# A four-layer graph network on one core: tiles finished in fours, column sums on ScalarE, and shifted transposes around the last layer

## The chip, the cores and the metric

The kernel runs on 1 core of a Trainium2 chip. The metric is the device time of one execution, in microseconds (us). Three runs of the kernel before gave 3246.93, 3250.04 and 3250.78 us: the median is 3250.04. Lower is better.

The engines are called by the names of the profile: PE (TensorE, matmul; PEld is its weight load), DVE (VectorE), ACT (ScalarE), POOL (GpSimd) and SP (SyncE, which here only issues DMAs). Each engine works off its own queue in order.

## The reference

An input x of 3327 rows by 512 columns and a 3327 x 3327 adjacency matrix pass through four layers. Each layer adds its result to its input and normalises every row:

```python
x = _layernorm(x + _L0_gnn_ref(x, adj, W, a))   # attention, 8 heads of 64
x = _layernorm(x + _L1_gnn_ref(x, adj, ..., 64)) # mean over the first 64 neighbours, two linear maps
x = _layernorm(x + _L2_gnn_ref(x, adj, W, a))   # attention, 8 heads of 64, then elu
x = _layernorm(x + _L3_gnn_ref(x, adj, W, a))   # attention, 4 heads of 128, then elu
```

An attention layer projects x to Wh, takes for each head e[i, j] = leaky_relu(f1[i] + f2[j]) where adj[i, j] > 0, a softmax over j, and sums Wh[j] with these weights.

## The kernel before, in words

The 3327 rows are 26 tiles of 128 (NT = 26, the last one short by one row), in two halves of 13 tiles (HALF). The program is one stream of stages:

- the first projection (x times W of layer 0), during which most of the adjacency matrix is loaded as int32 and turned into a one-byte mask. The mask is made in pieces of 128 rows by 832 columns: `mask_load` (L885) issues the load from SP, `mask_set` (L894) makes the mask on DVE, or for some later ones on ACT. The pieces of the first half of the columns, and those of the second half for the first EARLY row tiles, belong to this stage (L1415, L1416); the others are made one by one during the first unit of the layer 0 attention, 4/3 of a step per row tile (`some`, L1494);
- the layer 0 attention (`attention8`), layer 1 (`sage`), the layer 2 attention (`attention8`);
- `third` (L1205): the layer 2 rows are finished and projected to layer 3, then the layer 3 attention (`attention`, `unit`) runs, with the finishing of the output as side jobs.

An attention unit loops over the 26 row tiles j: DVE makes t (L430 or L709), ACT makes y from it (L435 or L710), PE multiplies t with the values into `po` and y and the mask into `pd` (denominators). After the loop `po` is moved out to `ob`, and work on it is put in a list of jobs, of which the next unit takes one per row tile. At the end of three of layer 3's eight units (the fourth of the first half, the second and third of the second half) the denominators leave `pd` by four DVE block transposes (L529, L531), two DVE reduces (L535) and one store `dd` from SP; `place` (L540) loads them back in another layout by 16 small DMAs, and `finish_sums` (L555) makes the reciprocals `rec`.

Finishing rows (`finish_steps`, L167) works on a group of n tiles: a load of the attention's sums h and of the layer's input xr; for each tile a `divide` (h times `rec` on DVE, L183, and for an elu layer e = exp(h) on ACT, L190) and an `add` (two DVE instructions, L198 and L199); then `norm_rows` (L148) for the group: for each tile bn_stats and bn_aggr on DVE (L154, L155), one square root for the group on ACT (L156), one reciprocal and one product on DVE (L157, L160), and for each tile the scaling on ACT (L163). Each list of steps is called in the loop of `third`.

In that loop (L1236) the finished tile y is stored to x3 from SP, `project1` (L260) transposes it on PE into `pt`, ACT copies it to xT (L269), DVE sums the columns into xsum (L270, for the mean row used by the attention); `project2` (L273) of the tile before runs 16 matmuls into `pw`, and ACT and DVE take the result apart (rc, qc, dc, vt). Groups are of two tiles, loaded three groups ahead (`load_group`, L1226), with 10 buffers for h and 6 for xr. At tile 14 `prepare` (L306) and `cut` of the first half of layer 3 are put in. The layer 2 denominators come in by `L2.late`: `place` at tile 4, `finish_sums` at tile 8.

The order of PE's instructions is that of the program (L64). The order of the other engines' instructions is chosen when the program is built, by a planner with its own estimate of durations and landings: an instruction may be queued ahead of earlier written ones. `tc.keep_in_program_order(ins)` holds one instruction behind the one written just before it on the same engine. Pools with `bufs=k` rotate k buffers of one name; a tile waits until the one that had its buffer is no longer used.

Of the kernel before, what the change touches and what calls it, by code (L numbers as in the profile page):

```python
# [18 lines left out]
P = 128  # L19
# [13 lines left out]
def kernel(  # L33
# [23 lines left out]
    CUTS = ((0, WA // 2), (WA // 2, WA), (WA, WA + WB // 2), (WA + WB // 2, IW))  # L57
    assert WA // 2 <= 512
    PIECES = (0, 48, 72, 32)
    EARLY = 10  # L60
    QUADS = [(s, min(4, HALF - s)) for s in range(0, HALF, 4)]


# [81 lines left out]
            eng.dma_start(out=t[:, :, e, :FW], in_=src[:, e * FW:(e + 1) * FW].rearrange("(c p) m -> p c m", p=P))  # L145


    def norm_rows(pool, ys, t0):  # L148
        n = len(ys)
        st = pool.tile([P, 4, 6], F32, name="st")  # L150
        mv = pool.tile([P, 4, 2], F32, name="mv")
        rs = pool.tile([P, 4, 2], F32, name="rs")
        for s, y in enumerate(ys):
            nc.vector.bn_stats(out=st[:, s, :], in_=y)  # L154
            nc.vector.bn_aggr(out=mv[:, s, :], in_=st[:, s, :])  # L155
        nc.scalar.activation(rs[:, :n, 0], mv[:, :n, 1], AF.Sqrt, bias=eps)  # L156
        nc.vector.reciprocal(rs[:, :n, 0], rs[:, :n, 0])  # L157
        if t0 + n == NT:
            nc.vector.tensor_tensor(rs[:, n - 1, 0:1], rs[:, n - 1, 0:1], valid, op=ALU.mult)
        nc.vector.scalar_tensor_tensor(rs[:, :n, 1], mv[:, :n, 0], -1.0, rs[:, :n, 0],  # L160
                                       op0=ALU.mult, op1=ALU.mult)
        for s, y in enumerate(ys):
            nc.scalar.activation(y, y, AF.Identity, bias=rs[:, s, 1:2], scale=rs[:, s, 0:1])  # L163

    def finish_steps(pool, xin, layer, t0, n, hbufs=6, eng=nc.sync, xbufs=None, xpool=None, ebufs=None, pinned=False):  # L167
        H, D = layer.H, layer.D
        ys, xs, steps = [], [], []

        def load():
            for t in range(t0, t0 + n):
                xr = xpool.tile([P, F], F32, name="xr", tag="hb") if xpool else \
                    pool.tile([P, F], F32, name="xr", bufs=xbufs)
                h = pool.tile([P, F], F32, name="h", bufs=hbufs)
                load_tile(h, hd, t, eng)
                ys.append(h)
                load_tile(xr, xin, t, nc.gpsimd)
                xs.append(xr)

        def divide(s):
            h = ys[s]
            ins = nc.vector.tensor_tensor(h.rearrange("p (h d) -> p h d", h=H), h.rearrange("p (h d) -> p h d", h=H),  # L183
                                          rec[:, t0 + s, :H].rearrange("p (h e) -> p h e", e=1).to_broadcast([P, H, D]),
                                          op=ALU.mult)
            if pinned and t0 > 2:
                tc.keep_in_program_order(ins)
            if layer.elu:
                e = pool.tile([P, F], F32, name="e", bufs=ebufs)
                ins = nc.scalar.activation(e, h, AF.Exp)  # L190
                if pinned and layer.li == 2 and (t0, s) == (2, 0):
                    tc.keep_in_program_order(ins)
                xs.append(e)

        def add(s):
            h, xr = ys[s], xs[s]
            if layer.elu:
                nc.vector.scalar_tensor_tensor(xr, xs[n + s], 1.0, xr, op0=ALU.min, op1=ALU.add)  # L198
                nc.vector.scalar_tensor_tensor(h, h, 0.0, xr, op0=ALU.max, op1=ALU.add)  # L199
            else:  # L200
                nc.vector.tensor_tensor(h, h, xr, op=ALU.add)

        steps.append(load)
        if pinned:
            steps += [lambda s=s: divide(s) for s in range(n)] + [lambda s=s: add(s) for s in range(n)]
        else:
            for s in range(n):
                steps += [lambda s=s: divide(s), lambda s=s: add(s)]
        steps.append(lambda: norm_rows(pool, ys, t0))
        return ys, steps  # L210

    def finish(*a):
# [20 lines left out]
    class Layer:  # L233
# [25 lines left out]

        def project1(self, pool, ps, xt, t, blocks=False):  # L260
            xT = pool.tile([P, FC, P], F32, name="xT")
            if blocks:

                tc.keep_in_program_order(nc.vector.transpose(xT, xt))
            else:
                pt = ps.tile([P, FC, P], F32, name="pt")
                for c in range(FC):
                    nc.tensor.transpose(pt[:, c, :], xt[:, c * P:(c + 1) * P], ident)
                nc.scalar.copy(xT, pt)  # L269
            nc.vector.tensor_reduce(xsum[:, :, t], xT, AX.X, ALU.add)  # L270
            return xT
# [116 lines left out]
        def unit(self, pools, half, s, background, aside, final=None, ending=None, following=None):  # L388
# [135 lines left out]
            if not by_pe:  # L524


                end = half == 1 and s == NS - 1
                for c in range(2):
                    ins = nc.vector.transpose(db[:64, c * (WA // 2):(c + 1) * (WA // 2)], pd[c][:64, :WA // 2])  # L529
                    tc.keep_in_program_order(ins)  # L530
                    nc.vector.transpose(db[64:, c * (WB // 2):(c + 1) * (WB // 2)], pd[c][64:, :WB // 2])  # L531
                red = yp.tile([P, WA // 32, 2, NS], F32, name="red", tag="y")
                dv = db.rearrange("p (b s x) -> p b s x", s=NS, x=8)
                for o in range(2):
                    nc.vector.tensor_reduce(red[:, :, o, :], dv[:, :, :, 3 * o:3 * o + 3], AX.X, ALU.add)  # L535
                dd = dram.tile([P, WA // 32, 2 * NS], F32, name=f"dd{self.li}{half}{s}")
                nc.sync.dma_start(out=dd, in_=red.rearrange("p b o s -> p b (o s)"))
                held = []
# [12 lines left out]


                nc.vector.tensor_copy(rec[:, t0:t0 + HALF, hs], self.rc[:, t0:t0 + HALF, hs])

                def finish_sums():  # L555
                    pes = held[0]
# [15 lines left out]
                    return jobs  # L572
                if final and s > 1:

                    return [nothing, nothing, place, nothing, nothing, nothing, finish_sums] + jobs[2:]
# [629 lines left out]
    def third(first):  # L1205
        with tc.tile_pool(name="col3", bufs=1) as cp:
# [5 lines left out]
            with tc.tile_pool(name="p_w", bufs=1, reuse_waits="tile") as wp, \  # L1212
# [12 lines left out]

                def load_group(t0):  # L1226
                    if t0 < NT:
                        groups.append(finish_steps(fp, x2, L2, t0, 2, 10, nc.gpsimd if t0 < 4 else nc.sync, 6,
                                                    pinned=t0 == 2))
                        groups[-1][1].pop(0)()  # L1230

                load_group(2)
                load_wide(wsb, w3, nc.gpsimd)
                nc.vector.tensor_copy(wsb[:, :, :, FW:], wa[3].rearrange("p c (e h) -> p c e h", e=2))
                load_group(4)
                for t0 in range(0, NT, 2):  # L1236
                    ys = ahead
                    if t0 in (4, 8):
                        L2.late.pop(0)(fp)
                    load_group(t0 + 6)  # L1240
                    for s, y in enumerate(ys):
                        t = t0 + s
                        store_tile(x3, y, t, nc.sync)
                        xT = L3.project1(pp, ps, y, t)
                        if s == 0 and groups:
                            ahead, steps = groups.pop(0)
                            for f in steps:
                                f()
# [16 lines left out]
            with tc.tile_pool(name="f3", bufs=2) as fp, tc.tile_pool(name="f4", bufs=1) as gp:  # L1265
# [10 lines left out]
                def later(s):  # L1276
                    jobs = []
                    if s == 0:
                        jobs += [none] * 12
                        for t0 in range(0, HALF, 2):  # L1280
                            ys, steps = finish_steps(fp, x3, L3, t0, min(2, HALF - t0), 2)

                            def stores(ys=ys, t0=t0):
                                for q, y in enumerate(ys):
                                    store_tile(out, y, t0 + q, nc.sync)

                            jobs += steps + [stores]
# [111 lines left out]
    with tc.tile_pool(name="mask0", bufs=1, reuse_waits="tile") as mp0, \  # L1399
# [8 lines left out]
        with tc.tile_pool(name="p_w", bufs=1, reuse_waits="tile") as wp, \  # L1408
# [42 lines left out]
            for t in range(1, NT):  # L1451
                xT = L0.project1(pp, ps, load(t), t)
                L0.project2(pp, bank, wsb, *pend)
                pend = (xT, t)
                for _ in range(2 + (t % 3 == 1) if t < NT - 4 else 7):
                    if msteps:
                        msteps.pop(0)()
                if t == HALF + 1:
                    L0.prepare(pp, 0)
                    L0.cut(pp, 0)  # L1460
                if t == NT - 6:
                    L0.first_rows = L0.wide_rows(ring, UNITS[0])
# [115 lines left out]
```

## Time and profile before

| what | us |
|---|---|
| median of the runs (lowest, highest) | 3250.04 (3246.93, 3250.78) |
| the profiled execution, its own time | 3250.52 |
| its span, from the first instruction to the last | 3248.8 |
| PE busy in the span | 3139.2 (97%) |
| DVE busy | 2627.8 (81%) |
| ACT busy | 2286.6 (70%) |
| POOL busy | 233.5 (7%) |

The span by stages, with the busy time of the engines in each (from the windows of the trace):

| stage | from, to | length | PE | DVE | ACT |
|---|---|---|---|---|---|
| first projection | 0, 142 | 142 | 123.9 | 88.1 | 29.3 |
| layer 0 attention | 142, 945 | 803 | 795.3 | 780.1 | 714.1 |
| layer 1, projection of layer 2 | 945, 1613 | 668 | 654.9 | 369.5 | 257.4 |
| layer 2 attention | 1613, 2411 | 798 | 783.4 | 771.4 | 705.6 |
| last projection | 2411, 2551 | 140 | 117.5 | 113.0 | 102.9 |
| layer 3 attention | 2551, 3220 | 669 | 659.1 | 488.0 | 466.8 |
| last rows | 3220, 3249 | 29 | 5.2 | 17.8 | 10.5 |

How to read the profile: a page shows one execution; its busy times come from the hardware's record of each instruction. The slices cut the span in 40 parts of 81 us, each digit the busy share of an engine in tenths. A row of a timeline has the start, the length, the engine, the line, the operation, the operands, how many were merged, and in brackets how long the engine stood idle before it and which instruction ended that. A row of waits has who waited for whom, the sum in us, how often, and the longest. A row of windows has the stretch, its length and the busy time of each engine in it. A row of groups has line, engine, operation, operands, count, then busy us and mean ns, then idle time before. Matmuls are pipelined and their ends modelled, so a busy PE is not a PE at its best.

### The profile page before, as it was taken

What the parts mean: (1) busy time and instruction counts of PE and PEld (TensorE: products, weight loads), DVE (VectorE), ACT (ScalarE), POOL (GpSimd) and SP (SyncE); (2) the same over time, 40 slices, a digit from 0 to 9 for tenths busy, and PEclk for the clock granted to TensorE, in tenths of its full rate; (3) what the DMA queues carried; (4) which work ended last, traced back from release to release, by engine and by line L of the source; (5) the groups of instructions that cost most, each with busy time, mean ns of one, the idle gap of its engine ahead of it and who ended that gap; (6) DMA issues with size and microseconds to landing.
All of it is one profiled execution on the core that took longest, in us unless ns stands there. A gap on an engine that the chain in (4) does not pass through costs nothing.

```text
span 3248.8 us, 44852 instructions
## 1 busy us (share of the span) xinstructions
PE 3139.2 (97%) x17910; PEld 1601.2 (49%) x17910; DVE 2627.8 (81%) x2329; ACT 2286.6 (70%) x1817; POOL 233.5 (7%) x378
## 2 busy tenths in 40 slices
PE   8899999999999999999999999999988999999997
PEld 7644343333334467777633333333337655555453
DVE  5799999999977645555589999999989666677886
ACT  2398888899972334444488988899888655568886
POOL 3100000000010011111100000000011000010110
PEclk9999999999999999999999999999999999999998
DMA  9751114111134355555341111011137211122211
GB/s 365 263 175 52 43 53 154 40 42 41 33 110 125 96 136 133 141 132 153 93 134 45 42 35 38 20 42 41 32 107 244 80 43 43 44 57 89 85 42 52
DMA packets 354575, 300.07 MB, mean 92 GB/s; under 512 B 232420, under 2 KB 288174, under 8 KB 352831
## 3 DMA queue, kind: packets, MB, share of 16 engines
q1 hardware_dynamic: 322175, 185.92, 19.7%
q0 software_dynamic: 26672, 103.60, 10.1%
q10 hardware_dynamic: 5520, 7.69, 0.8%
q8 instruction: 141, 2.31, 0.3%
q14 instruction: 67, 0.55, 0.1%
HBM read 220.27 MB, written 76.84 MB: 91 GB/s over the span
## 4 chain that ended last, share of the span: by engine, by line
PE 81%; DVE 6%; issue 4%; DMA 4%; ACT 3%; POOL 0%; SPq 0%; POOLq 0%; DVEq 0%; ACTq 0%
PE po L731 35%; PE po L452 13%; PE acc L1171 9%; PE pd L687 7%; PE pw L278 6%; DVE t L709 3%; PE pz L1069 3%; PE pi L1072 3%; DMA raw<-in_adjT_dram 2%; PE pd L405 1%; PE pk L1040 1%; ACT y L435 1%; PE pt L751 1%; DVE t L430 1%; PE pe L793 1%
## 5 line engine op out<-in xcount | busy, mean ns | idle before, releaser
L710 ACT ACTIVATE y<-t,bi,sc 128x3328 fp8e4<-128x3328 f32 (+1 forms) x520 | 1337.4, 2603 | 105.0 <-PE pd L687 48.2
L731 PE MATMUL po<-t,vj 128*64 128x448 f32 (+1 forms) x6656 | 1276.2, 524 | 13.0 <-DVE t L709 12.0
L731 PEld LDWEIGHTS po<-t,vj 128*64 128x64 f32 x6656 | 457.7, 138 | 694.4 <-issue 631.0
L452 PE MATMUL po<-t,vj 128*128 128x448 f32 (+1 forms) x1664 | 601.8, 518 | 7.3 <-DVE ob L481 3.6
L430 DVE SCALAR_TENSOR_TENSOR t<-rba,qc,mk 128x1664 f32<-128x1664 f32 x208 | 403.4, 1946 | 131.0 <-PE po L452 97.6
L435 ACT ACTIVATE y<-t,bi,sc 128x1664 fp8e4<-128x1664 f32 x208 | 365.8, 1772 | 188.0 <-DVE t L430 174.2
L452 PEld LDWEIGHTS po<-t,vj 128*128 128x128 f32 x1664 | 312.0, 191 | 277.9 <-issue 172.8
L709 DVE SCALAR_TENSOR_TENSOR t<-rba,qc,mk 128x3328 f32<-128x3328 f32 (+1 forms) x130 | 379.6, 2987 | 12.8 <-DMA mk<-md 8.4
L709 DVE SCALAR_TENSOR_TENSOR t<-rbb,qc,mask 128x3328 f32<-128x3328 f32 (+1 forms) x130 | 380.0, 2984 | 10.2 <-PE po L731 7.2
L709 DVE SCALAR_TENSOR_TENSOR t<-rbb,qc,mk 128x3328 f32<-128x3328 f32 (+1 forms) x130 | 379.3, 2984 | 10.3 <-PE po L731 8.9
L709 DVE SCALAR_TENSOR_TENSOR t<-rba,qc,mask 128x3328 f32<-128x3328 f32 (+1 forms) x130 | 380.7, 2985 | 6.9 <-PE po L731 6.1
L1171 PE MATMUL acc<-zs,kt 128*128 128x512 f32 x1352 | 360.2, 420 | 0.0
L278 PE MATMUL pw<-wsb,xT 128*128 128x264 f32 (+1 forms) x1248 | 299.3, 395 | 10.3 <-DVE vt L284 8.2
L1171 PEld LDWEIGHTS acc<-zs,kt 128*128 128x128 f32 x1352 | 255.6, 189 | 52.2 <-PE pk L1022 0.8
L687 PE MATMUL pd<-y,sden 128*32 128x384 fp8e4 (+1 forms) x3328 | 271.6, 344 | 0.0
L278 PEld LDWEIGHTS pw<-wsb,xT 128*128 128x128 f32 x1248 | 239.9, 196 | 53.2 <-ACT xT L269 6.2
L1029 ACT CAST pk<-cy 128x512 f32<-128x512 bf16 x169 | 99.1, 587 | 221.4 <-DVE kt L1043 214.8
L1043 DVE SCALAR_TENSOR_TENSOR kt<-pk,mb 128x512 fp32r<-128x512 f32 x169 | 115.5, 684 | 116.7 <-PE pk L1040 115.5
L687 PEld LDWEIGHTS <-sden 128*32 128x32 bf16 x3328 | 89.7, 95 | 165.7 <-issue 150.1
L284 DVE TENSOR_TENSOR vt<-pw,dc 128x256 f32<-128x256 f32 x156 | 59.0, 417 | 71.1 <-ACT dc L279 66.0
L1069 PE MATMUL pz<-wn,xT 128*128 128x512 f32 x208 | 96.3, 607 | 5.7 <-DMA wn<-in_wnT_dram 5.4
L999 POOL DMA_DIRECT2D cy<-ctd x91 | 67.9, 746 | 368.1 <-ACT pk L1029 300.8
(221 smaller groups left out, 2080.1 us busy)
## 6 DMA issues: line engine op xcount, KB each, us to landing
raw<-in_adjT_dram SPq DMA_DIRECT2D x67, 416.0 KB
vj<-v SPq DMA_DIRECT2D x156, 128.0 KB
cy<-ctd POOLq DMA_DIRECT2D x78, 256.0 KB, 4.2
h<-hd SPq DMA_DIRECT2D x61, 256.0 KB
v<-vt SPq DMA_DIRECT2D x50, 256.0 KB
xr<-x POOLq DMA_DIRECT2D x45, 256.0 KB, 3.3
md<-mask SPq DMA_DIRECT2D x26, 416.0 KB
mb<-md SPq DMA_DIRECT2D x169, 64.0 KB
```

The costliest lines, as they stand in the source:

```text
L278: nc.tensor.matmul(pw[e][:, :FW + H], xT[:, c, :], wsb[:, c, e, :], start=c == 0, stop=c == FC - 1)
L430: ins = nc.vector.scalar_tensor_tensor(t, rb[k], self.qc[:, j, h:h + 1], mask_at[0](j, i0, IW), op0=ALU.max, op1=ALU.mult)
L435: nc.scalar.activation(y, t, AF.Sigmoid, bias=self.bi[:, j, h:h + 1], scale=self.sc[:, j, h:h + 1], saturate=False)
L452: nc.tensor.matmul(po[c][k * D:(k + 1) * D, :z - a_], vj[:, j % 2, k * D:(k + 1) * D], ts[k][:, a_:z], start=j == 0, stop=j == NT - 1)
L687: nc.tensor.matmul(pd[c][32 * kk:32 * kk + 32, :w_], lhsT, rhs, start=(kk, c) not in seen, stop=last and j == NT - 1)
L709: nc.vector.scalar_tensor_tensor(to, ro, self.qc[:, j, h:h + 1], m, op0=ALU.max, op1=ALU.mult)
L710: nc.scalar.activation(yo, to, AF.Sigmoid, bias=self.bi[:, j, h:h + 1], scale=self.sc[:, j, h:h + 1], saturate=False)
L731: nc.tensor.matmul(po[c][k * D:(k + 1) * D, :z - a_], vj[:, j % 2, x_:x_ + D], t[:, k, a_:z], start=j == 0, stop=j == NT - 1)
L1029: nc.scalar.copy(pks[k % 2], carry[b, t // 4 * 4][:, t % 4:t % 4 + 2, :])
L1043: nc.vector.scalar_tensor_tensor(kt, pk, NEIGHBOURS, mb[:, t:t + 2, :], op0=ALU.is_le, op1=ALU.mult)
L1069: nc.tensor.matmul(pz, xT[:, c, :], wn[:, c, :], start=c == 0, stop=c == FC - 1)
L1171: nc.tensor.matmul(acc, kts[b, t][:, s * P:(s + 1) * P], zs(t, c), start=t == 0 and c == 0, stop=t == NT - 1 and c == 1)
```

## The change

- `EARLY` goes from 10 to 8, so four mask pieces leave the first projection for the layer 0 attention; in the last four tiles of that stage the number of mask steps per tile goes from 7 to 4, 7, 4, 7.
- `norm_rows` can pin its reciprocal, and does so for tile 0 of layer 2. `divide` of layer 2 is pinned in every group called with `pinned`, which are now the groups at tiles 2 and 4 (before: an exp of the group at tile 2 alone).
- In `third` the tiles from 6 on are finished in groups of four, with all divides of a group written ahead of its adds (`together`), h in 14 buffers and xr in 12. A group's steps are spread over the first three tiles of the group before it. `place` and `finish_sums` of layer 2 are called at tiles 2 and 6.
- `project1` of layer 3 copies xT by four ACT instructions of 128 columns each, whose accumulator output is the column sum; the DVE reduce for xsum is gone there.
- In `unit` the block transposes of `pd`, the reduces and the store `dd` become the first two jobs of the next unit, without the pin, in place of two empty jobs.
- In the side jobs of the layer 3 attention the divides of a pair are written ahead of its adds.

The diff, cut to its core:

```diff
-    EARLY = 10
+    EARLY = 8
...
-    def norm_rows(pool, ys, t0):
+    def norm_rows(pool, ys, t0, pinned=False):
...
-        nc.vector.reciprocal(rs[:, :n, 0], rs[:, :n, 0])
+        ins = nc.vector.reciprocal(rs[:, :n, 0], rs[:, :n, 0])
+        if pinned:
+            tc.keep_in_program_order(ins)
...
-            if pinned and t0 > 2:
+            if pinned and (t0 > 2 or layer.li == 2):
                 tc.keep_in_program_order(ins)
...
-        if pinned:
+        if pinned or together:
             steps += [lambda s=s: divide(s) for s in range(n)] + [lambda s=s: add(s) for s in range(n)]
...
-        steps.append(lambda: norm_rows(pool, ys, t0))
+        steps.append(lambda: norm_rows(pool, ys, t0, t0 == 0 and layer.li == 2))
...
             xT = pool.tile([P, FC, P], F32, name="xT")
+            if self.li == 3:
+                pt = ps.tile([P, FC, P], F32, name="pt")
+                for c in range(FC):
+                    nc.tensor.transpose(pt[:, c, :], xt[:, c * P:(c + 1) * P], ident)
+                for c in range(FC):
+                    nc.scalar.activation(xT[:, c, :], pt[:, c, :], AF.Copy, accum_out=xsum[:, c, t:t + 1])
+                return xT
...
-                for c in range(2):
-                    ins = nc.vector.transpose(db[:64, c * (WA // 2):(c + 1) * (WA // 2)], pd[c][:64, :WA // 2])
-                    tc.keep_in_program_order(ins)
+                def blocks(c):
+                    nc.vector.transpose(db[:64, c * (WA // 2):(c + 1) * (WA // 2)], pd[c][:64, :WA // 2])
                     nc.vector.transpose(db[64:, c * (WB // 2):(c + 1) * (WB // 2)], pd[c][64:, :WB // 2])
...
+                jobs[:2] = [lambda: blocks(0), lambda: blocks(1)]
...
-                        groups.append(finish_steps(fp, x2, L2, t0, 2, 10, nc.gpsimd if t0 < 4 else nc.sync, 6,
-                                                    pinned=t0 == 2))
+                        groups.append(finish_steps(fp, x2, L2, t0, 2 if t0 < 6 else 4, 14, nc.gpsimd if t0 < 4 else nc.sync,
+                                                   12, pinned=t0 < 6, together=True))
...
                 load_group(4)
-                for t0 in range(0, NT, 2):
+                load_group(6)
+                t = -1
+                for t0 in (0, 2, 4, *range(6, NT, 4)):
                     ys = ahead
-                    if t0 in (4, 8):
+                    if t0 in (2, 6):
                         L2.late.pop(0)(fp)
-                    load_group(t0 + 6)
+                    load_group({2: 10, 4: 14}.get(t0, t0 + 12 if t0 >= 6 else NT))
+                    steps = []
+                    if groups:
+                        ahead, steps = groups.pop(0)
+                    per = -(-len(steps) // max(1, len(ys) - 1)) if len(ys) > 2 else len(steps)
                     for s, y in enumerate(ys):
                         t = t0 + s
                         store_tile(x3, y, t, nc.sync)
                         xT = L3.project1(pp, ps, y, t)
-                        if s == 0 and groups:
-                            ahead, steps = groups.pop(0)
-                            for f in steps:
-                                f()
+                        for f in steps[per * s:per * (s + 1)]:
+                            f()
...
-                            ys, steps = finish_steps(fp, x3, L3, t0, min(2, HALF - t0), 2)
+                            ys, steps = finish_steps(fp, x3, L3, t0, min(2, HALF - t0), 2, together=True)
...
-                for _ in range(2 + (t % 3 == 1) if t < NT - 4 else 7):
+                for _ in range(2 + (t % 3 == 1) if t < NT - 4 else 4 + t % 2 * 3):
```

More of the change, by code (lines that the diff above doesn't have):

```diff
@@ L163, in norm_rows, with finish_steps @@
             nc.scalar.activation(y, y, AF.Identity, bias=rs[:, s, 1:2], scale=rs[:, s, 0:1])
-    def finish_steps(pool, xin, layer, t0, n, hbufs=6, eng=nc.sync, xbufs=None, xpool=None, ebufs=None, pinned=False):
+    def finish_steps(pool, xin, layer, t0, n, hbufs=6, eng=nc.sync, xbufs=None, xpool=None, ebufs=None, pinned=False,
+                     together=False):
         H, D = layer.H, layer.D
@@ L527, in unit @@
                 end = half == 1 and s == NS - 1
-                for c in range(2):
-                    ins = nc.vector.transpose(db[:64, c * (WA // 2):(c + 1) * (WA // 2)], pd[c][:64, :WA // 2])
-                    tc.keep_in_program_order(ins)
+                dd = dram.tile([P, WA // 32, 2 * NS], F32, name=f"dd{self.li}{half}{s}")
+                held = []
+                def blocks(c):
+                    nc.vector.transpose(db[:64, c * (WA // 2):(c + 1) * (WA // 2)], pd[c][:64, :WA // 2])
                     nc.vector.transpose(db[64:, c * (WB // 2):(c + 1) * (WB // 2)], pd[c][64:, :WB // 2])
[L532 to L538, printed above, removed]
+                    if c == 0:
+                        return
+                    red = yp.tile([P, WA // 32, 2, NS], F32, name="red", tag="y")
+                    dv = db.rearrange("p (b s x) -> p b s x", s=NS, x=8)
+                    for o in range(2):
+                        nc.vector.tensor_reduce(red[:, :, o, :], dv[:, :, :, 3 * o:3 * o + 3], AX.X, ALU.add)
+                    nc.sync.dma_start(out=dd, in_=red.rearrange("p b o s -> p b (o s)"))
+                    nc.vector.tensor_copy(rec[:, t0:t0 + HALF, hs], self.rc[:, t0:t0 + HALF, hs])
+                jobs[:2] = [lambda: blocks(0), lambda: blocks(1)]
                 def place(eng=nc.gpsimd):
@@ L550, in place @@
                                 tc.keep_in_program_order(ins)
-                nc.vector.tensor_copy(rec[:, t0:t0 + HALF, hs], self.rc[:, t0:t0 + HALF, hs])
                 def finish_sums():
@@ L573, in unit @@
                 if final and s > 1:
-                    return [nothing, nothing, place, nothing, nothing, nothing, finish_sums] + jobs[2:]
+                    return jobs[:2] + [place, nothing, nothing, nothing, finish_sums] + jobs[2:]
                 jobs += [nothing] * max(0, 7 - len(jobs))
```

## The prediction

> **What bounds the kernel now.** I read the slices first, then a table of windows by stage, then TensorE's waits, then the timelines where it waits. From the page:
>
> ```profile
> PE   8899999999999999999999999999988999999997
> DVE  5799999999977645555589999999989666677886
> ACT  2398888899972334444488988899888655568886
> ```
>
> TensorE (PE) is nearly full everywhere except at the start and in slices 28 to 30, so only a stage in which it waits can give time back. All that this change touches lies in three such places: the first projection (0 to 142 us), the last projection, and the unit boundaries of the last attention (2551 to 3220). The windows of the last projection, which starts when the previous attention's last transpose ends at 2414.9 (columns: busy us of PE, PEld, DVE, ACT, POOL; granted clock; DMA share; GB/s):
>
> ```profile
> 2414.90:2425.00 10.10, 0.57 (x4) 0.55 (x4) 4.69 (x11) 3.26 (x5) 0.92 (x2) 0.63 0.98 338
> 2425.00:2455.00 30.00, 25.08 (x110) 19.91 (x109) 28.56 (x63) 24.59 (x49) 7.71 (x12) 0.90 0.79 243
> 2455.00:2505.00 50.00, 43.73 (x213) 36.72 (x212) 46.90 (x134) 40.64 (x85) 4.84 (x9) 0.93 0.73 233
> 2505.00:2551.00 46.00, 45.72 (x227) 39.46 (x227) 29.38 (x62) 32.44 (x69) 1.06 (x2) 1.00 0.38 137
> ```
>
> PE idles for ten microseconds, then VectorE (DVE) is 95% busy up to 2505 and PE waits; only the last window is PE's own. An undisturbed tile costs 3.945 us (transposes at 2512.38, next at 2516.33), so 26 tiles need 102.6 us, plus 2.3 for 13 `pr` transposes and 3.6 for the mean: 108.5. It takes 136.5 (2414.9 to 2551.4). **28 us are lost here.** PE's waits:
>
> ```profile
> PE pt L268 <- ACT h L163: 15.1, 5, 9.5
> PE pr L325 <- ACT rr L327: 4.0, 1, 4.0
> ```
>
> The first row is transposes waiting for a normalised tile. Its longest wait, 9.5, explains itself in the DVE timeline:
>
> ```profile
> 2415.80 0.18 DVE L155 BATCH_NORM_AGGREGATE mv<-st 128x2 f32<-128x6 f32 x1
> 2417.22 0.69 DVE L183 TENSOR_TENSOR h<-h,rec 128x512 f32<-128x512 f32 x1 [1.24 <-DMA h<-hd]
> 2421.51 0.69 DVE L183 TENSOR_TENSOR h<-h,rec 128x512 f32<-128x512 f32 x1 [3.60 <-DMA h<-hd]
> 2422.59 0.69 DVE L183 TENSOR_TENSOR h<-h,rec 128x512 f32<-128x512 f32 x1 [0.38 <-DMA h<-hd]
> 2423.20 0.16 DVE L157 RECIPROCAL rs<-rs 128x2 f32<-128x2 f32 x1
> ```
>
> ScalarE (ACT) had the square root ready at 2416.8, but the reciprocal of tiles 0 and 1 stands in DVE's queue behind the divisions of tiles 3, 4 and 5, which wait for their loads. PE starts at 2424.45.
>
> **What the Trainium skill says.** "ScalarE: Activation LUTs", section "Table sets: the hidden batching unit", asks for all activations of one table set before the next, since each switch reloads the table. Here Sqrt and Exp alternate once per group:
>
> ```profile
> L156 ACT ACT_TABLE_LOAD x13 | 16.7, 1283 | 0.5 <-DVE mv L155 0.3
> L279 ACT ACT_TABLE_LOAD x8 | 10.3, 1283 | 0.1
> L190 ACT ACT_TABLE_LOAD x7 | 9.0, 1283 | 0.1
> ```
>
> 28 loads are 36 us of ACT's 101 in the stage. The page, under "What ACT_TABLE_LOAD costs", adds a drain of about 1.38 us to each; the trace shows the Exp following its load by 0.01 us (load 2407.74 for 1.28, Exp 2409.03), so I go by the trace's 1.28. Second, "TensorE: Matmul & The Clock Gate", section "Part 1: The HAM clock gate", says an idle array drops to half clock and wins it back only after sustained work. The trace agrees: 16 `pw` matmuls after the 4.0 us wait took 5.48 us against 3.67, so a long wait costs 1.8 us more than it shows. I go by that row.
>
> **The change, part by part.**
>
> *Head of the last projection.* `keep_in_program_order` holds an instruction behind the one written before it on its engine: the pinned L824 ran at 2423.58, right behind L160 at 2423.39, its unpinned twin at 2411.47. Pinning the reciprocal behind its own bn_aggr says little alone. But the divisions of tiles 4 and 5 are now pinned too, and the vector instruction written before them is `vt` of tile 1. So they leave the reciprocal's way. Those of 2 and 3 may stay ahead (3 waits till 2417.22), so: reciprocal 2417.9, L160 2418.1, first normalise to 2419.1 instead of 2424.4. **−5.3 us.** The w3 load lies before this: issued at 2406.2 and 2407.0, 4.7 us at most to landing.
>
> *Tiles 2 to 5.* Queued behind the now waiting division of tile 4 are that group's exps, adds and norm. PE's 32 matmuls of tiles 0, 1 took 9.26 us cold: from about 2421 to 2429.3 (estimate). `vt` of tile 1 follows at 2431.5, after an Exp table load (1.28). Then two divisions 1.3, first exp 0.6, four adds 2.4, two stats 1.2, Sqrt with its load 1.6, reciprocal 0.4, normalise 0.8: tile 4 at 2439.4. Tiles 2, 3 are ready by 2430 (divided by 2418, their exps behind xT of tile 0), so the old wait of 2.46 goes; PE does pw of tile 2 to 2435.2 and waits 4.2 for tile 4, plus 1.8 cold. That replaces 0.95, 0.20 and 0.58 for tiles 4 to 6. I get pw of tile 5 at 2449.9, against 2454.4 now: **−4.5 with the head**, so this part alone is +0.8.
>
> *Tile 5 to the end.* DVE's column sums go: 26 x 0.68 = 17.7 us (0.60 spacing, 15.6 off the queue). Per tile DVE then does 0.6 + 1.2 + 0.7 + 0.7 = 3.2 us against 3.8, under PE's 3.945. Groups of four bring 13 Sqrts down to 8, so about 10 table loads fewer, 13 us of ACT. Against it, one 0.59 us copy becomes four of 128 columns with a sum. Nearest row: `hb` 128x128, 0.265 us; four are 1.06. The sum's own price shows nowhere: nothing at the low end, another small ACT instruction (`rc`, 0.16) per column block at the high end. I take 0.09, about the overlap of two copies. ACT per tile: exp 0.63, normalise 0.81, copies 1.4, dc/rc/qc 0.48, a quarter of Sqrt and two loads 0.72: 4.0 by durations, about 3.4 when successive ones overlap by 0.09. Just under PE. So of what PE loses after tile 5 now (2.0 at tile 12; 0.3 + 4.0 + 1.8 cold at `pr`, where `rr` copies stood behind table loads) I count **−5** and leave 3 at `pr`. A group of four takes about 11 us of DVE, spread over the four tiles before it (15.8 us), so it is covered once the stage runs; with only two exp buffers exps 3, 4 wait for adds 1, 2, inside that cover. The deeper h and xr buffers only let loads start earlier: POOL's xr waits (43.4 us) hide already.
>
> *Place and sums of layer 2* come one group earlier: 16 `pes` DMAs of 0.56 us on SP, 9 us of queue in which x3 stores and the loads of tiles 10 to 13 stand, which PE wants 25 us later; and ten DVE instructions of 0.2. Nothing, while h loads stay that far ahead.
>
> *First projection, EARLY 8.* Four pieces of 416 KB leave the stage (1.7 MB, 4.7 us at 364 GB/s). But from 116 us to 139.5 the chain is PE's own, and its waits before (8.2 us on `vt`) come earlier than the thinned tail: 0, at best −4. They return as one set in unit 0, where DVE is the chain (0.5 us), and three in unit 1, where PE is: +0.5.
>
> *Last attention.* The four pd transposes (2.5 us) and reduces (1.0) move into the next unit's first two jobs. They are written before its third `t` as now, so their order on DVE may not alter: 0, at best the 3.1 us PE waits for `t` in this stage, at worst +2 if `dd` leaves late and sums hold DVE (it stood 3.9 us for pes at 3154, hidden). Divisions paired in the later jobs: some Exp loads saved beside a full PE. Together −1.
>
> **Sum:** −4.5 −5 +0.5 −1 = −10 on a span of 3248.8, so 3238.8; the profiled execution took 3250.5 with 1.7 around its span and lies 0.5 above the median of 3250.04. Predicted: **3240**.
>
> **Rivals.** *Slower: loads ahead of the reciprocal again.* The divisions of tiles 6 to 9 are not pinned. If one of them is queued before the reciprocal, it waits for h rows that SP issues from 2416.2 on; at the 8.9 us that tile 5 took, the fourth lands near 2428, five microseconds after today's reciprocal. Then +4.8 at the head, the tile 4 stall on top (6.0 for 4.2 of old waits), +1 for layer 3: 3257 with nothing won later. For: DVE really ordered four divisions so. Against: SP has two hb stores between. It decides when that division ends past 2423.2. *No change: ACT becomes the bound.* At the high price a tile costs ACT 4.3 by durations, 0.4 over PE for 20 tiles: +8, so 3248. For: ACT was 81% busy to 2505. Against: 13 us of table loads go. *Better:* tile 4's stall does not arise (the transposes of `t` and the first stage give a little too): 3229. *The pins do nothing*, the order stays, but DVE is lighter: 3245, in the no-change case.
>
> **How the numbers follow.** Forecast (3233 to 3243.5) 0.54; better 0.12; no change, the two cases with it, 0.19; slower 0.15. By the bound of 0.2%, 6.5 us, about what a measurement of this kernel can tell from none: faster 0.66, same 0.19, slower 0.15. The range reaches to 3229 and 3254, leaving out half of the better case and half of the slower one.
>
> **What would show it.** Right: the reciprocal near 2418; PE's first `pt` wait near 4; one wait at tile 4; 18 or so table loads; the stage near 127 us; DVE without L270. Wrong: a division with a DMA wait ahead of the reciprocal; PE waiting on `xT`; column sums over 0.4 us each; PE's idle in the last attention (2551 to 3220) above today's 9.9 us.

## The result and the profile after

The kernel after takes 3259.59 us (median of 6 runs, 3258.11 to 3264.49), beside 3250.14 us for the kernel before in the same series (6 runs): the ratio is 1.0034, 95% interval 1.0021 to 1.0047. The forecast was 3240 with a range to 3254; it is slower, by 9.5 us between the medians.

The profiled execution took 3264.49 us, its span is 3262.8. It lies 5 us above its own median, and differs by 6.5 us in one stretch that the change does not touch: from 1499 us on, a stretch of layer 1 takes 16.1 us in place of 9.6 (PE waits 4.0 us for `kt` there, before 0.27). Of the 14 profiled executions of this study seven took 9.6 to 10.5 there and seven 14 to 17, in no relation to what was changed. What makes it so stays open; the comparisons by stage leave it out, medians may differ by a few us for it alone.

| stage in us (between the same PE instructions) | before | after | forecast of the change |
|---|---|---|---|
| start to the second unit's first tiles (the 1641st matmul) | 278.1 | 286.2 | +0.5 |
| last projection, end of the attention's last transpose to the last matmul | 136.7 | 143.5 | −9.5 |
| layer 3 attention, up to PE's last transposes | 675.0 | 669.6 | −1 |

The slices after, beside those shown of before:

```profile
PE   8899999999999999999989999999987999999997
DVE  5798999999977645555499999999988566677887
ACT  1398888899873334444388988899887655568886
```

The hole of the last projection is still there: slices 30 and 31 read 8 and 7, before 8 and 8. Its windows, cut in the same way (busy us of PE, PEld, DVE, ACT, POOL; clock; DMA share; GB/s):

```profile
2427.80:2438.00 10.20, 6.54 (x20) 5.23 (x20) 3.08 (x8) 6.02 (x22) 2.35 (x2) 0.67 0.42 123
2438.00:2468.00 30.00, 17.44 (x72) 14.15 (x71) 19.98 (x44) 16.87 (x52) 10.48 (x20) 0.77 0.92 311
2468.00:2520.00 52.00, 43.42 (x204) 36.30 (x204) 47.23 (x130) 41.67 (x154) 3.76 (x7) 0.93 0.63 212
2520.00:2571.00 51.00, 50.84 (x257) 44.17 (x258) 22.41 (x52) 34.45 (x145) 1.26 (x3) 1.00 0.41 145
```

PE now starts early (6.54 us busy in the first ten, 0.57 before), but in the next thirty it works 17.4 us in place of 25.1, and VectorE works less too (20.0 in place of 28.6). What runs there is DMA: 0.92 of the engines, 311 GB/s, in place of 0.79 and 243. In the first window it was at 0.42 and 123 GB/s, in place of 0.98 and 338. The loads have moved later, into the stage. PE's waits in the stage say the same:

```profile
PE pt L268 <- ACT h L165: 20.8, 4, 11.0
PE pr L335 <- ACT rr L337: 1.7, 1, 1.7
```

Four waits for a normalised tile, 20.8 us in place of 15.1. The PE timeline places them:

```profile
2431.02 1.97 PE L268 MATMUL pt<-ident,h 128*128 128x128 f32 x8 [3.20 <-ACT h L165]
2433.45 9.40 PE L288 MATMUL pw<-wsb,xT 128*128 128x260 f32 x32 [0.46 <-ACT xT L270]
2453.82 1.97 PE L268 MATMUL pt<-ident,h 128*128 128x128 f32 x8 [10.97 <-ACT h L165]
2456.91 6.11 PE L288 MATMUL pw<-wsb,xT 128*128 128x260 f32 x16 [1.12 <-ACT xT L270]
2462.86 0.60 PE L268 MATMUL pt<-ident,h 128*128 128x128 f32 x4
2463.29 3.67 PE L288 MATMUL pw<-wsb,xT 128*128 128x260 f32 x16
...
2476.55 1.12 PE L268 MATMUL pt<-ident,h 128*128 128x128 f32 x4 [4.93 <-ACT h L165]
```

The head is right: 3.20 us in place of 9.53. The 10.97 us ahead of tile 2 are new. Behind them 16 matmuls take 6.11 us, and the next 16 take 3.67: the wait costs 2.4 us more than it shows. The granted clock is 0.57 from 2453.8 to 2463.0 and 1.00 in the seven us behind, which agrees with the Trainium skill, "TensorE: Matmul & The Clock Gate", section "Part 1: The HAM clock gate", that an array that stood idle runs at half its clock at first.

Why is tile 2 late? VectorE after:

```profile
2429.76 0.17 DVE L157 RECIPROCAL rs<-rs 128x2 f32<-128x2 f32 x1 [1.35 <-ACT rs L156]
...
2431.49 0.96 DVE L843 TENSOR_REDUCE red<-db 128x112 f32<-128x336 f32 x2
2440.62 0.76 DVE L294 TENSOR_TENSOR vt<-pw,dc 128x256 f32<-128x256 f32 x2 [8.17 <-ACT dc L289]
2441.34 0.69 DVE L186 TENSOR_TENSOR h<-h,rec 128x512 f32<-128x512 f32 x1
```

The reciprocal comes at once, no division ahead of it. But the first division of the stage comes 11.6 us later, behind `vt` of tile 0. Its data is not there sooner. GpSimd's queue before, and then after:

```profile
2411.11 0.55 POOL L128 DMA_DIRECT2D h<-hd  x1 [3.39 <-ACT e L190]
...
2415.41 0.44 POOL L346 MEMSET pc<- 128x416 bf16 x1
2429.22 2.01 POOL L255 MEMSET sden<- 128x2288 bf16 x1 [13.37 <-DMA hd<-hb]
```

```profile
2420.65 0.44 POOL L356 MEMSET pc<- 128x416 bf16 x1
2435.65 2.01 POOL L258 MEMSET sden<- 128x2288 bf16 x1 [14.55 <-DMA hd<-hb]
2437.60 0.79 POOL L260 MEMSET sm<- 128x832 bf16 x1
2438.34 0.55 POOL L128 DMA_DIRECT2D h<-hd  x1
```

Before, tile 2's h was asked for 3.8 us ahead of the stage's start (2414.9), and the memset of `sden`, which waits for the attention's last stores, came behind it. After, the memset is first in the queue, and h is asked for 10.5 us behind the start (2427.8). The loads of tiles 4 to 9 on SP follow at 2439.9, behind nine of the sixteen `pes` loads.

The memory plan of the two programs gives a reason. A load into a buffer has to wait until whatever lay on that memory is no longer used. In the last unit of layer 2's attention, t lies from byte 130208 to 170144 of each partition, y from 170144 to 180128, v and the last `hb` above that. Ahead of h in the pool lie 6 xr buffers before, 12 after. Tiles 3 to 7 have their h from 150688 to 160928 before, over t only. After, they lie from 171168 to 181408, over y and `hb`, which PE and the last store use to the end of the attention. Tile 2's own buffer lies over t in both, but its load is queued right in front of tile 3's; why the planner holds it back as well is not shown. This is the theory to be tested: **the deeper buffers moved h onto memory that comes free late.** The rivals: groups of four, the pinned divisions, or the sums on ScalarE cost the time.

The second loss is at 265 us, one row of VectorE and one of PE:

```profile
265.12 0.60 DVE L914 TENSOR_SCALAR mask<-raw 128x831 fp8e4<-128x831 int32 x1 [4.73 <-DMA raw<-in_adjT_dram]
```

```profile
269.36 4.71 PE L743 MATMUL po<-t,vj 128*64 128x448 f32 x16 [3.35 <-DVE t L721]
```

A mask set that the lower EARLY moved into the second unit of layer 0 waits for its piece, with that unit's t behind it in the queue. The rival here: a chance of this one execution.

### The profile page after: what moved, and what is told of

Read it like the earlier page. It is cut to its first block, busy times and chain, and to the rows that moved or that the text cites. A ratio compares the mean times of both kernels' runs of the same rounds, so it can differ in the third digit from the quotient of the medians.

```text
span 3262.8 us, 44961 instructions
## 1 busy us (share of the span) xinstructions
PE 3142.4 (96%) x17910; PEld 1603.4 (49%) x17910; DVE 2610.0 (80%) x2291; ACT 2285.1 (70%) x1984; POOL 233.2 (7%) x378
## 5 line engine op out<-in xcount | busy, mean ns | idle before, releaser
L743 PE MATMUL po<-t,vj 128*64 128x448 f32 (+1 forms) x6656 | 1277.8, 525 | 16.1 <-DVE t L721 15.1
```

Of the source, the lines that this page charges most:

```text
L743: nc.tensor.matmul(po[c][k * D:(k + 1) * D, :z - a_], vj[:, j % 2, x_:x_ + D], t[:, k, a_:z], start=j == 0, stop=j == NT - 1)
```

## The experiments

Each kernel was timed against the kernel before (5 to 22 runs of it); a ratio below is to the kernel before, with its 95% interval. A figure for a wait or a stage comes from the one profiled execution. "Kernel 8" is the kernel of experiment 8. "Stage" is the last projection, measured as in the table above (before 136.7, after 143.5).

**1. The mask part taken back.** `EARLY = 10` and 7 mask steps per tile in the tail, in the kernel after.

> The kernel after with the mask part of the change taken back: EARLY is 10 again and the last four tiles of the first projection take 7 mask steps each. Theory (mask sets moved into the second unit of the layer 0 attention stand in VectorE's queue for their load): the wait of 4.7 us at 265 us of the trace and the cold matmuls behind it go, and so do about 1.5 us in the first projection; the time is 6 to 8 us below the kernel after, about 3252. Rival (the difference of the first 280 us is a chance of one profiled execution): the median stays at 3259 and only the place of the waits changes.

Measured: 1.0005 (0.9997 to 1.0013), 3250.76 us. The start takes 280.5 us (after 286.2, before 278.1), the wait at 265 us is gone, and the last projection keeps its 143.1. The ratio stands 0.0029 below that of the kernel after, some 9 us: more than the expected 6 to 8, but two series are compared, and the trace shows 5.7. The theory holds against its rival, chance; the size is known to a few us only.

**2. Fewer buffers.** In the kernel after:

```diff
-  finish_steps(fp, x2, L2, t0, 2 if t0 < 6 else 4, 14, nc.gpsimd if t0 < 4 else nc.sync, 12, ...
+  finish_steps(fp, x2, L2, t0, 2 if t0 < 6 else 4, 12, nc.gpsimd if t0 < 4 else nc.sync, 8, ...
```

> The kernel after with 12 buffers for h in place of 14 and 8 for xr in place of 12; nothing else changes, the groups of four, the pins and the column sums stay. The buffers of the first h tiles then lie 12 KB lower in each partition, on memory that held only t of the layer 2 attention, not its y and its last hb. Theory (the first loads of the last projection came late because their buffers lay on memory that the attention used to its end): the loads of tiles 2 to 9 are issued before the stage starts, the wait of 11 us at tile 2 and that of 5 us at tile 6 fall to some 2 to 4 us together, the stage takes about 128 us in place of 143, and the time is about 3245. Rival (groups of four, the pinned divisions or the sums on ScalarE cost the time): the stage stays at 140 us or more and the time at 3256 to 3260.

Measured: 1.0000 (0.9992 to 1.0009), 3247.70 us; the stage takes 134.0. Tiles 2 to 7 have their h between 144544 and 169120 here, over t only, and GpSimd asks for tile 2 at 2407.53, 7 us ahead of the stage's start, the memset behind it. PE:

```profile
2417.95 1.97 PE L268 MATMUL pt<-ident,h 128*128 128x128 f32 x8 [3.20 <-DMA xr<-x]
...
2433.12 1.36 PE L268 MATMUL pt<-ident,h 128*128 128x128 f32 x8 [3.48 <-ACT h L165]
...
2447.02 1.11 PE L268 MATMUL pt<-ident,h 128*128 128x128 f32 x4 [7.32 <-ACT h L165]
2447.93 5.55 PE L288 MATMUL pw<-wsb,xT 128*128 128x260 f32 x16
```

Of the stage, 9.5 us come back by the buffer counts alone. The expected 128 is not reached: a wait of 7.32 us now stands at tile 4, where the prediction had 4.2.

**3. The address alone.** In the kernel before, pairs and its 10 and 6 buffers kept:

```diff
+                nc.vector.memset(fp.tile([P, 5120], F32, name="pad", bufs=1)[:, :1], 0.0)
                 load_group(2)
```

> The kernel before with one unused tile of 20 KB per partition (one element of it is written) ahead of the h and xr buffers in the pool of the last projection; the counts of buffers stay 10 and 6 and the groups stay pairs. The first h tiles then get the addresses that they have in the kernel after. Theory (address alone): the first h loads are queued behind the sden memset on GpSimd and start about 10 us after the stage does; the reciprocal of tiles 0 and 1 comes early by itself, because the divisions that stood ahead of it have no data yet (some 5 us won), then tiles 2 to 9 come late (some 12 to 18 us lost): the time is 6 to 13 us above the kernel before, 3256 to 3263. Rival (the loads are late because of the groups of four or of the earlier place of the denominators): within 3 us of the kernel before, 3247 to 3253.

Measured: 1.0019 (1.0012 to 1.0025), 3254.71 us; the stage takes 141.4. An unused tile makes this kernel slower by 6 us. GpSimd:

```profile
2423.89 2.01 POOL L255 MEMSET sden<- 128x2288 bf16 x1 [14.59 <-DMA hd<-hb]
2425.83 0.79 POOL L257 MEMSET sm<- 128x832 bf16 x1
2426.57 0.55 POOL L128 DMA_DIRECT2D h<-hd  x1
```

and PE:

```profile
2419.23 1.97 PE L268 MATMUL pt<-ident,h 128*128 128x128 f32 x8 [3.21 <-ACT h L163]
...
2442.30 1.97 PE L268 MATMUL pt<-ident,h 128*128 128x128 f32 x8 [11.56 <-ACT h L163]
```

The same queue and the same pair of waits as after (3.20 and 10.97), without a group of four, a pin or a sum on ScalarE. That settles that addresses alone make the loads late; that it is `y` and `hb` which hold them is read from the memory plan. It shows something else: the head is short here without any pin, because the divisions have no data to stand in front with. In the kernel after the pins were not needed for it.

**4, 5. The layer 3 parts**, in the kernel before: both, then the block transposes as jobs alone.

> The kernel before with the two parts of the change that touch the layer 3 attention: the block transposes of pd as the first jobs of the next unit, and the divides of a pair ahead of its adds in the side jobs. Theory (the 6 us won in that stage come from these parts): 4 to 6 us below the kernel before, 3244 to 3246. Rival (they come from a different order of VectorE's queue that the rest of the change brings about): within 2 us of the kernel before, about 3250.

> The kernel before with one of the two parts in the layer 3 attention: the block transposes of pd, the reduces and the store as the first two jobs of the next unit; divides and adds of the side jobs as before. Theory (the blocks stood in VectorE's queue ahead of t where PE waits at a unit's start): 2 to 4 us of the 4.5 us won there come from it, all at the boundaries with such blocks; the stage is 260 to 261.5 us between its marks in place of 263.6. Rival (the pairing of divides with one Exp table load wins it all): the stage stays within 1 us of 263.6.

Measured: both 0.9996 (0.9988 to 1.0004), 3248.28 us; the blocks alone 0.9984 (0.9977 to 0.9990), 3243.61 us. By the traces they are alike: layer 3 takes 670.5 and 670.7 (before 675.0), and from 2962.8 of the kernel before, the marks of the second expectation, 259.1 and 259.2 in place of 263.6. In the traces the blocks win it all, 4.3 to 4.4 us, slightly more than was expected of them, and the paired divides nothing. The timing of "both" does not show the gain; its interval leaves room for 4 us, and whether the paired divides cost something elsewhere stays open. Half of the gain comes at one boundary. VectorE before:

```profile
3053.63 0.59 DVE L531 STREAM_TRANSPOSE db<-pd 64x384 f32<-64x384 f32 x1
...
3054.86 0.94 DVE L535 TENSOR_REDUCE red<-db 128x112 f32<-128x336 f32 x2
...
3056.39 1.93 DVE L430 SCALAR_TENSOR_TENSOR t<-rba,qc,mk 128x1664 f32<-128x1664 f32 x1
```

with the blocks alone:

```profile
3056.81 0.59 DVE L534 STREAM_TRANSPOSE db<-pd 64x384 f32<-64x384 f32 x1
3057.43 1.95 DVE L431 SCALAR_TENSOR_TENSOR t<-rba,qc,mk 128x1664 f32<-128x1664 f32 x1
...
3059.38 0.48 DVE L540 TENSOR_REDUCE red<-db 128x112 f32<-128x336 f32 x1
```

The transposes stand ahead of the same t in both, but the reduces now stand behind it. PE's wait for that t falls from 2.52 to 1.89 us, the 16 matmuls behind it from 7.55 to 5.93: 2.2 us in all. Another 1.6 come near 3137, where a wait of 1.42 for y goes; there the side work ahead of the boundary is in another order, which was not taken apart.

**6, 7. The sums and the pins, each alone**, in the kernel before: `project1` as in the change; and the three pins as in the change, with pairs and 10 and 6 buffers.

> The kernel before with the column sums of layer 3 moved to ScalarE as in the change (four copies of 128 columns with an accumulator output in place of one copy and VectorE's reduce); pairs, buffers, order of steps and everything else as before. Theory (VectorE sets the pace from 2425 to 2505 us, so 16 to 18 us less of it there count in part): the last projection is 4 to 8 us shorter than before, about 3243. Rival (ScalarE's longer copies, about 0.45 us more per tile, put off the normalised tiles and the head is unchanged): within 2 us of before, 3248 to 3250.

> The kernel before with the pins of the change alone: the reciprocal of tiles 0 and 1 held behind its statistics, and the divisions of the groups at tiles 2 and 4 held in program order; pairs, buffers and VectorE's column sums as before, and the h loads start as early as before. Theory (the pinned divisions of tiles 4 and 5 wait for vt of tile 1 and put tile 4 off): the first transposes of the last projection start 5 to 6 us earlier, then a wait of 5 to 8 us with cold matmuls at tile 4 gives most of it back: the stage is 0 to 3 us shorter, 3246 to 3249. Rival (the head's gain stays, as the sum had it): 4 to 5 us shorter, 3244.

Measured: sums 1.0010 (1.0002 to 1.0019), 3251.17 us, stage 136.3: the theory fails and the rival holds, there is no gain. The head still waits 9.38 us, and a wait of 4.57 stands at tile 6. Pins 1.0002 (0.9993 to 1.0010), 3248.60 us, stage 135.9: as the first theory had it, the head waits 3.21, then tile 2 waits 5.24 and tile 4 5.81.

**8. The parts together**: the kernel before with pins, sums and the layer 3 parts; pairs, 10 and 6 buffers, EARLY 10 and the denominators at tiles 4 and 8 stay.

> The kernel before with those parts of the change that leave the h loads and the first projection alone: the pins, the column sums on ScalarE and the two parts in the layer 3 attention; pairs, 10 and 6 buffers, EARLY 10 and the denominators at tiles 4 and 8 as before. Theory (the parts are worth what the single runs show, and only the buffers and the mask part cost): last projection 5 to 9 us and layer 3 attention 4 us shorter, 3236 to 3241. Rival (the pins give back at tile 4 what they win, and the rest overlaps): 3242 to 3246.

Measured: **0.9965 (0.9952 to 0.9977), 3236.68 us**, below both kernels. The stage takes 129.7, layer 3 669.5. Sums and pins win 0.4 and 0.8 us of the stage alone and 7.0 together. PE's waits in the stage:

```profile
PE pt L268 <- ACT h L165: 9.2, 2, 6.2
PE pt L268 <- DMA xr<-x: 3.7, 1, 3.7
```

Tile 2 waits 3.01 of these and tile 4 6.19. In the order of this program VectorE has the divisions of tiles 6, 7 and 8, which no pin holds, ahead of tile 2's adds, and stands there for their loads:

```profile
2430.78 2.00 DVE L186 TENSOR_TENSOR h<-h,rec 128x512 f32<-128x512 f32 x3 [4.25 <-DMA h<-hd]
```

**9. The same with fewer pins**: `pinned=t0 == 2` in place of `pinned=t0 < 6`, so the divisions of tiles 4 and 5 are free; the reciprocal's pin stays.

> The parts together once more, but with the division pins on the group at tile 2 alone, so that the divisions of tiles 4 and 5 are free; the reciprocal keeps its pin. Theory (the pin on the divisions of tiles 4 and 5 moves the wait from the reciprocal to tile 4): these divisions stand ahead of the reciprocal again, the head wait is near 9 us in place of 3.7 and the wait at tile 4 (6.2 us) nearly goes; the time is 1 to 5 us above the parts together, 3238 to 3242. Rival (the pin on the reciprocal wins the head by itself): head wait stays under 5, wait at tile 4 goes too, 3231 to 3233.

Measured: 0.9996 (0.9987 to 1.0004), 3246.22 us, stage 137.0: 9.5 us above the parts together, more than expected, of which the stage shows 7.3. VectorE:

```profile
2416.02 0.69 DVE L186 TENSOR_TENSOR h<-h,rec 128x512 f32<-128x512 f32 x1 [1.47 <-DMA h<-hd]
2418.12 0.69 DVE L186 TENSOR_TENSOR h<-h,rec 128x512 f32<-128x512 f32 x1 [1.41 <-DMA h<-hd]
2420.40 0.69 DVE L186 TENSOR_TENSOR h<-h,rec 128x512 f32<-128x512 f32 x1 [1.59 <-DMA h<-hd]
2421.01 0.16 DVE L157 RECIPROCAL rs<-rs 128x2 f32<-128x2 f32 x1
```

The divisions are back in front of the pinned reciprocal; the head waits 8.77 and, as with the sums alone, tile 6 waits 4.57. So it is the pins on the divisions of tiles 4 and 5 that the head needs, once the loads are early; what the reciprocal's own pin adds was not tried.

**10. The denominators later**, in kernel 2, which has 12 and 8 buffers: `if t0 in (4, 6)` in place of `(2, 6)` for `L2.late`.

> The kernel with 12 and 8 buffers once more, and in it the 16 loads of the denominators placed at tile 4 in place of tile 2 (the sums stay at tile 6, since tiles 10 to 13 need them). Theory (the 16 small loads stand in SP's queue for some 10 us ahead of h loads that tiles 7 to 9 wait for): the divisions stop waiting for h at 2438 us of its trace, the wait at tile 4 (7.3 us there) falls below 5, and the last projection is 2 to 5 us shorter than with 12 and 8 buffers, about 3244. Rival (the wait at tile 4 is that of the pinned divisions behind vt of tile 1): the wait at tile 4 stays at 6 us or more and the time at 3247.

Measured: 0.9990 (0.9983 to 0.9997), 3245.56 us; the stage takes 131.5, 2.5 less; the wait at tile 4 falls from 7.32 to 4.64. So the earlier place was not free.

**11. Groups of four with the rest mended**: kernel 10 with EARLY 10.

> The kernel after with 12 and 8 buffers, the 16 loads of the denominators at tile 4, and the mask part taken back (EARLY 10). What it has beyond the kernel with the parts together is the groups of four with their steps spread over three tiles, the deeper buffers and the earlier place of the denominators. Theory (with the loads early again the groups of four are worth nothing: the waits are at tiles 2 and 4, ahead of the first group of four): last projection within 3 us of the parts together, the time 3237 to 3241. Rival (fewer table loads and fuller groups help behind tile 6, once the rest is out of the way): 3232 to 3235.

Measured: 0.9978 (0.9970 to 0.9986), 3241.97 us; stage 131.9, against 129.7 for the pairs of kernel 8. The groups of four win nothing that shows over pairs; as the theory had it, the waits lie ahead of the first of them.

**12. The mask part alone**, in the kernel before.

> The kernel before with the mask part of the change alone: EARLY 8 and the last four tiles of the first projection take 4, 7, 4, 7 mask steps. Theory (a mask set of the second unit stands in VectorE's queue for its load): one wait of about 4 us on t, and cold matmuls behind it, at the start of the second unit near 264 us, 5 to 6 us in all: 3254 to 3256. Rival (that wait belongs to the rest of the change): within 2 us of before, 3247 to 3251.

Measured: 1.0016 (1.0009 to 1.0024), 3253.40 us, and the row is there again:

```profile
263.72 0.60 DVE L902 TENSOR_SCALAR mask<-raw 128x831 fp8e4<-128x831 int32 x1 [4.58 <-DMA raw<-in_adjT_dram]
```

PE then waits 3.19 for t. The mask part costs about 5 us by itself.

The steps from the parts together to the kernel after, in order (a ratio is known to about 0.001):

| kernel | ratio to before | stage | what was added |
|---|---|---|---|
| 8, parts together | 0.9965 | 129.7 | |
| 11 | 0.9978 | 131.9 | groups of four, 12 and 8 buffers, sums at tile 6 |
| 10 | 0.9990 | 131.5 | mask part |
| 2 | 1.0000 | 134.0 | denominators' loads at tile 2 |
| after | 1.0034 | 143.5 | 14 and 12 buffers |

## Why the prediction was wrong

- *"The deeper h and xr buffers only let loads start earlier"*: **The step that failed.** They made the loads start later: 9.5 us of the stage (143.5 against 134.0), 0.0034 of the time. A buffer's address decides what it waits for, and the prediction never asked where the new ones would lie. For the stage 127.2 was forecast and 143.5 came: 9.5 of these 16.3 us are the addresses, 2.5 the place of the denominators' loads, and 4.3 were too much hoped for even without both (131.5, kernel 10).
- *Place and sums: "Nothing, while h loads stay that far ahead."* They did not stay ahead; even with early loads it costs 2.5 us (kernels 2 and 10).
- *First projection, +0.5.* Kernel 12 shows +5.3 (interval 2.9 to 7.8). The prediction counted the instructions of the moved pieces, not the wait of a set for its load with a t queued behind it.
- *Head, −5.3.* Near: −6.3, from 9.53 to 3.20. The reason was right where loads are early (kernel 9 undoes it). In the kernel after itself it came about in part by luck: there the late loads alone would have given it (kernel 3).
- *Tiles 2 to 5, "this part alone is +0.8".* The place was right, the size was not. In kernel 8, with early loads, tile 2 waits 3.01 (forecast: gone) behind the divisions of tiles 6 to 8, and tile 4 6.19 (forecast 4.2); the pins alone leave 0.8 us of the head's 6.3. The slower rival named unpinned divisions of tiles 6 to 9 in VectorE's way; they do stand there, one group later than it said.
- *Tile 5 to the end, −5.* From tile 6's transposes to the middle of tile 15's projection, kernel 8 needs 45.5 us against 53.5, −8.0, and even the kernel after is at 50.3. But the column sums, named as the reason, win 1.9 of it alone and the pins 5.9 (51.6 and 47.6). ScalarE did not become the bound; PE's waits for xT are 1.6 us in the stage after. The 18 table loads came as forecast (30 before), but kernel 8 has 30 too and is faster: the ScalarE time that fewer loads free won nothing that shows.
- *Last attention, −1.* It is −5.4 after; the blocks alone win 4.3 to 4.4. That "their order on DVE may not alter" held for the transposes and not for the reduces, which a t now passes; the bound named for the best case, 3.1, was too low: it counted PE's waits for `t` only, and the matmuls behind a shorter wait were faster too (5.93 for 7.55).
- *The slower rival* ended near the measured time, but by another road: no division stood ahead of the reciprocal. A number that fits does not make its mechanism right.

For kernel 8 the sum over its own parts would have been −4.5 −5 −1 = −10.5, against 0.0035 of the time, 11 us, measured (interval 7 to 16). That it fits is in part luck, since two errors cancel: the stage won 7.0 us in place of 9.5, layer 3 some 5.5 in place of 1. The three things costed at nothing or at 0.5, addresses, place and mask part, lost 0.0056, some 18 us (table above).

Why sums and pins each win so little alone shows in part, by where the stage is longer. From its start to tile 6's transposes it takes 38.3 us before, 42.8 with the pins, 40.3 with the sums, 39.5 with both: each part loses ahead of tile 6 most of what it wins behind it. With the sums alone, as in kernel 9, PE waits 4.57 us at tile 6. There the divisions of tiles 11 and 12 stand ahead of tile 6's adds and wait for their loads; the sums alone:

```profile
2446.81 0.69 DVE L183 TENSOR_TENSOR h<-h,rec 128x512 f32<-128x512 f32 x1 [1.38 <-DMA h<-hd]
2448.84 0.69 DVE L183 TENSOR_TENSOR h<-h,rec 128x512 f32<-128x512 f32 x1 [1.34 <-DMA h<-hd]
```

In kernel 8 they stand behind these adds. No run held them back alone, and why the pins cost less ahead of tile 6 with the sums on ScalarE stays open.

## What to carry to other kernels

More buffers in a pool that takes over another stage's memory need not be free: see what each new address held and when that comes free, because here one late release put a whole queue of loads behind a memset. An edit costed at "nothing, while the loads stay ahead" needs the row that keeps them ahead looked at again under the change. Parts that win little alone can win together, so judge them in the combination, and undo them one by one from there.

## What the runs showed of the hardware

A ScalarE copy with an accumulator output is two records, here of the kernel after (group; count; busy us, mean ns; idle before):

```profile
L270 ACT ACTIVATE xT<-pt 128x128 f32<-128x128 f32 x104 | 27.3, 283 | 2.1 <-PE pt L268 2.0
L270 ACT ACTIVATION_READ_ACCUMULATOR xT<-pt 128x1 f32 x104 | 22.3, 215 | 0.0
```

They overlap: in kernel 2 four copies start 0.25 us apart (2433.82, 2434.08, 2434.33, 2434.58), so a tile takes about 1.0 us against 0.59 for the one copy of 512 columns.

What a wait of PE costs behind it does not follow from its length alone: behind waits for tile 2 of 2.46 us (kernel before), 2.56 (kernel 9) and 3.01 (kernel 8) the 16 matmuls of tile 2 took 3.77, 5.38 and 3.69 us.
